# Products of constants ahead of stages and between router products in a four-layer macaron network

## The chip, the cores and the metric

The kernel runs on one core of a Trainium2 chip. The metric is the device time of one execution in microseconds; the time of a kernel is the median of several runs. All data are 32-bit floats.

## What is computed

The reference passes a tensor x of 2 x 512 tokens with 256 features through four layers. Each layer is a feed-forward part, a sequence-mixing part and the same feed-forward part again, each behind a layer norm and added to x, the feed-forward parts at half weight. The parts are:

- Layer 0, feed-forward: a mixture of 32 experts of hidden size 176, 6 for each token, beside a shared gated network of hidden size 352. Sequence part: retention with 16 heads, and a GELU network.
- Layer 1, feed-forward: a linear layer with binarized weights. Sequence part: attention over the keys of those tokens that an importance score selects. The kernel does the whole layer in one stage, l1.
- Layer 2, feed-forward: 8 dense experts, of which the router picks one. Sequence part: a state-space mixer with 8 heads.
- Layer 3, feed-forward: a mixture of 8 experts of hidden size 176, 2 for each token, beside a shared network of hidden size 176. Sequence part: a state-space mixer with 64 heads.

The mixture of experts, which runs four times (twice in layer 0, twice in layer 3), is in short:

```python
scores = softmax(x2d @ wg_router.T)          # layer 3: sigmoid
topk_w, topk_idx = top_k(scores, K)
topk_w = topk_w / (sum(topk_w) + 1e-20)
g = einsum('ecd,edf->ecf', xe, w_gate)        # xe: the tokens of each expert
u = einsum('ecd,edf->ecf', xe, w_up)
ye = einsum('ecf,efd->ecd', silu(g) * u, w_down)
y = weighted sum of each token's K rows of ye
sh = silu(x2d @ ws_gate) * (x2d @ ws_up) @ ws_down
```

## The kernel before, in words

**Tiling.** The 1024 tokens are 8 chunks of 128 (NC = 8, four for each of the two sequences, CB = 4); the 256 features are two blocks of 128 (KD = 2). x stays in the on-chip memory throughout. Each 32-bit product that the program writes is two matmuls in the profile; a transpose, which is a product with the identity matrix, is one. The stages run one after the other, as STAGES lists them (L2072): l0_ffn, l0_attn, l0_ffn, l1, l2_ffn, l2_attn, l2_ffn, l3_ffn, l3_attn, l3_ffn.

**A mixture of experts (moe, L622).** For each sequence, layernorm (L221) makes xn on DVE from a mean and a scale that DVE and POOL work out (L201, L212), xn goes to a table in HBM, and transpose_tokens (L173) turns it with 8 transposes into ps_tr, from which DVE or ACT copies to xT. Then logits (L312) does the router: 8 chunks x 2 feature blocks, into ps_lg, and a DVE copy takes it out (L320). While DVE makes the lists of tokens, shared_unit (L354) runs the shared network, pg and pu first (L365), with DVE's h behind (L369). In this part the order of PE's instructions is the order in which they are written: in_order (L135) chains them.

Then experts_sparse (L506) runs the experts. A unit is an expert with one or two tiles of 128 tokens. POOL gathers the tokens from the table (xe, L527), turn_x (L537) transposes them (ps_xe, L541), hidden does gate and up (ps_gu, L551), turn_h transposes the result (ps_he, L565), down_ multiplies it by the last weight (ps_ye, L576), and POOL writes the rows to HBM (L581). The loop is pipelined over units: turn_x of unit n, turn_h of n - 2, hidden of n - 1, down_ of n - 2. A conditional branch (L688) holds further tiles for an expert that has more tokens than expected; it isn't entered here. The rows of a token are added to x only when the next stage needs them: settle (L159) runs add_rows (L694), which loads y<-rows and adds with DVE (L714) or, in l1, with PE into ps_add (L707).

**The stages behind a mixture of experts.** l0_attn (L767) begins with a norm by chunks (scales, norm), transposes pt_h (L833) and the projections pq. l1 (L1100) begins with add_rows through PE (ps_add), and a loop over chunks that are three steps apart. The state-space mixer (mamba, L1562) serves l2_attn (flag few, 8 heads) and l3_attn (64 heads). It has row (the norm and transposes of one sequence; in l3_attn by_chunks, L259, which takes each chunk as its rows come), decay_sums (L1605: pd, ps_row, ps_cum, ps_dec), convolutions whose projections pp (L1675) PE makes and whose taps DVE adds, products (L1699: pb, pm), prep_front and prep_back (pt, L1757), and z_gate (pz, L1809). The order of its start on PE, ACT and DVE is written out by hand from L1937 on, with in_order around it.

**PSUM.** In the mixture of experts' first part, and in l1 and the mixer, psM has 4 buffers under the tag "mm" that all small products take in turn; the experts have a pool with one buffer for each name.

**Constants.** ident is the 128 x 128 identity, le a 128 x 512 array of zeros and ones; both are loaded once at the start.

Of the kernel before, what the change touches and what calls it, by code (L numbers as in the profile page):

```python
# [10 lines left out]
F32 = mybir.dt.float32  # L11
# [7 lines left out]
P = 128  # L19
B, S, D = 2, 512, 256  # L20
T = B * S
NC = T // P
CB = S // P
# [60 lines left out]
class Net:  # L84
# [69 lines left out]
    def rsqrt(self, out, in_, scale=1.0):  # L154

        self.nc.scalar.activation(out, in_, AF.Sqrt, bias=self.eps, scale=scale)
        self.nc.vector.reciprocal(out, out)

    def settle(self, b, n=CB, psum=None):  # L159


        parts = self.pending.get(b, [])
        while len(parts) > CB - n:
            parts.pop(0)(psum)
        if not parts:
            self.pending.pop(b, None)
# [66 lines left out]
    def layernorm_T(self, es, psum):  # L233


        xT = es.enter_context(self.tc.tile_pool(name="xT", bufs=1)).tile([P, KD, T], F32, name="xT")
        p = es.enter_context(self.tc.tile_pool(name="ln", bufs=1))

        made = {}

        def measure(b):
            made[b] = self.scales(p, b)

        def norm(b):
            made[b] = self.layernorm(p, p.tile([P, CB, D], F32, tag="xn", name="xn"), b, *made[b])

        def turn(b, k):
            self.transpose_tokens(made[b], xT, psum, b, k)

        def row(b):  # L250
            if b in self.pending:
                by_chunks(b)
                return
            measure(b)
            norm(b)
            for k in range(KD):
                turn(b, k)

        def by_chunks(b):  # L259

            xn = p.tile([P, CB, D], F32, tag="xn", name="xn")
            ps = [psum.tile([P, S], F32, tag="mm", name="ps_tr") for _ in range(KD)]
            ms = {}
            for cc in range(CB + 1):
                if cc < CB:
                    self.settle(b, cc + 1)
                    ms[cc] = self.scale(p, b * CB + cc, b * CB + cc)
                if cc > 0:
                    j = cc - 1
                    self.centre(xn[:, j, :], b * CB + j, *ms[j])  # L270
                    for k in range(KD):
                        self.nc.tensor.transpose(
                            ps[k][:, j * P : (j + 1) * P], xn[:, j, k * P : (k + 1) * P], self.ident
                        )
            for k in range(KD):
                self.evac(xT[:, k, b * S : (b + 1) * S], ps[k])

        return xT, row, measure, norm, turn
# [30 lines left out]
        nc.vector.tensor_tensor(gt, gt, eq, ALU.add)  # L309
        return gt  # L310

    def logits(self, pool, psum, xT, wT, e):  # L312
        lg = pool.tile([P, NC, e], F32, name="lg")
        ps = psum.tile([P, NC, e], F32, tag="mm", name="ps_lg")
        for c in range(NC):
            for k in range(KD):
                self.nc.tensor.matmul(  # L317
                    ps[:, c, :], xT[:, k, c * P : (c + 1) * P], wT[:, k, :], start=(k == 0), stop=(k == KD - 1)
                )
        self.nc.vector.tensor_copy(lg, ps)  # L320
        return lg

# [183 lines left out]
    def experts_sparse(self, ew, ps, xes, table, rows, lists, w, ex, f, tiles, per, ahead=4, wp=None):  # L506
# [28 lines left out]
            return xe  # L535

        def turn_x(n, xe, nt):  # L537
            pt = ps.tile([P, KD, nt * P], F32, name="ps_xe")
            for k in range(KD):
                for i in range(nt):  # L540
                    nc.tensor.transpose(pt[:, k, i * P : (i + 1) * P], xe[:, i, k:D:KD], self.ident)  # L541
            xeT = ew.tile([P, KD, nt * P], F32, name=f"xeT{n % 2}")
            self.evac(xeT, pt)
            return xeT
# [25 lines left out]
        def down_(n, e, js, hT, wd):  # L570
            nt = len(js)
            y = ew.tile([P, nt, D], F32, name=f"ye{n % 4}")
            py = ps.tile([P, nt, D], F32, name=f"ps_ye{n % 2}")
            for i in range(nt):
                for q in range(2):
                    nc.tensor.matmul(  # L576
                        py[:, i, :], hT[:, q, i * P : (i + 1) * P], wd[:, q, :], start=(q == 0), stop=(q == 1)
                    )
            self.evac(y, py)
            for i, j in enumerate(js):  # L580
                put_rows = nc.gpsimd.indirect_dma_start(  # L581
                    rows,
                    bass.IndirectOffsetOnAxis(put[:, e * per + j : e * per + j + 1], 0),
                    y[:, i, :],
                    None,
                    bounds_check=last,
                    oob_is_err=False,
                )

                for other in self.puts:  # L590
                    self.tc.declare_no_dep(put_rows.ins, other.ins, reason="no two slots have one row")
                self.puts.append(put_rows)
# [29 lines left out]
    def moe(self, pre, names, E, F, K, FS, PER, tiles, cap, r, scores, scale):  # L622
# [6 lines left out]
        with ExitStack() as es:  # L629
# [7 lines left out]
            with ExitStack() as fs:  # L637
# [6 lines left out]
                with tc.tile_pool(name="ln", bufs=1) as lp:  # L644
                    tv = table[:, :D].rearrange("(b c p) d -> b p c d", p=P, b=B)
                    rT = self.router_weights(sb, psM, router, E)
                    tail = {}
                    with self.in_order(tail, ("PE",)):
                        for b in range(B):
                            xn = lp.tile([P, CB, D], F32, name=f"xn{b}")  # L650
                            self.layernorm(lp, xn, b, *self.scales(lp, b))
                            nc.scalar.dma_start(tv[b], xn)
                            for k in range(KD):
                                self.transpose_tokens(xn, xT, psM, b, k)
                        s = self.logits(sb, psM, xT, rT, E)
                if cap < T:

                    zero = lists.tile([P, D], F32, name="zero")
# [108 lines left out]
    def l0_attn(self):  # L767
# [10 lines left out]
        with ExitStack() as es:  # L778
# [252 lines left out]
                    nc.vector.tensor_tensor(self.x[:, c, :], self.x[:, c, :], py, ALU.add)  # L1031


            for c in range(2):
                scales(c)
            norm(0)
            w2 = self.w("fc1")[:, : KD * F].rearrange("p (k f) -> p k f", k=KD)
            nc.sync.dma_start(w2, a[pre + "fc1_w"].rearrange("(k p) f -> p k f", p=P))
            w3 = self.w("fc2")[:, : NF * D].rearrange("p (c d) -> p c d", d=D)
# [60 lines left out]
    def l1(self):  # L1100
# [19 lines left out]
        with ExitStack() as es:  # L1120
# [173 lines left out]


            with tc.tile_pool(name="a1m", bufs=4, space=PSUM) as psM:
                for c in range(NC + 4):
                    if c < NC:
                        front(c)
                    if c == CB:  # L1300
                        wt = self.w("w4")[:, : KD * 4 * D].rearrange("p (k n d) -> p k n d", k=KD, n=4)
                        for n, name in enumerate(("Wq", "Wk", "Wv", "Wo")):
                            nc.sync.dma_start(wt[:, :, n, :], a[pre + name].rearrange("(k p) d -> p k d", p=P))
                    if 0 <= c - 1 < NC:
                        turn_x(c - 1)
                    if 0 <= c - 2 < NC:
                        back(c - 2)
                    if 0 <= c - 3 < NC:
                        measure(c - 3)
                    if c >= 4:  # L1310
                        norm(c - 4)
                    if c == 1:
                        nc.gpsimd.tensor_copy(wib, wi.to_broadcast([P, KD, P]))
                        nc.vector.tensor_scalar(bqs, bq, DH**-0.5, None, ALU.mult)
                    if c == CB + 4:
                        importance(0)
                        for m in range(KD):
                            queries(0, m)
                    elif c > CB + 4:
                        for i in range(2):  # L1320
                            if 2 * (c - CB - 5) + i < CB:
                                ranks(0, 2 * (c - CB - 5) + i)
# [239 lines left out]
    def mamba(self, pre, win, wout, nh):  # L1562
# [14 lines left out]
        with ExitStack() as es:  # L1577
# [27 lines left out]
            def decay_sums(b):  # L1605
# [29 lines left out]
                nc.vector.tensor_scalar(t1, d, 1e-18, None, ALU.max)  # L1635
                nc.scalar.activation(jb[:, bs, :], t1, AF.Ln)
                yield

                cr = wk.tile([nh, 2, S], F32, tag="cr", name="cr", bufs=1)
                ps = psM.tile([nh, S], F32, tag="mm", name="ps_row")  # L1640
# [56 lines left out]
                return conv(wb[:, :, P : 2 * P], NX + 1, b, CT[:, b * S : (b + 1) * S])  # L1697

            def products(b):  # L1699
                pb = psM.tile([P, CB, P], F32, tag="mm", name="pb")  # L1700
                pm = psM.tile([P, CB, P], F32, tag="mm", name="pm")
                for cc in range(CB):
# [49 lines left out]
                return taps, rest  # L1752

            def prep_back(u, m):
                pt = psM.tile([P, CB, P], F32, tag="mm", name="pt")
                for cc in range(CB):
                    nc.tensor.transpose(pt[:, cc, :], u["xc"][:, m, cc * P : (cc + 1) * P], self.ident)  # L1757
                nc.scalar.copy(u["xt"][:, :, m * P : (m + 1) * P], pt)  # L1758

                n = u["g"] * NM + m  # L1760
                nc.scalar.mul(u["xc"][:, m, :], u["xc"][:, m, :], dcol[:, n : n + 1])
# [173 lines left out]
            later = {}  # L1935
            tail = {}
            with self.in_order(tail, ("PE", "Activation", "DVE")):  # L1937
                row(0)
                fetch_wx(*order[0])
                d0, d1 = decay_sums(0), decay_sums(1)  # L1940
# [178 lines left out]
```

## Time and profile before

| | us |
|---|---|
| median of three runs | 2031.36 (2030.21 to 2033.29) |
| the profiled execution | 2029.85 |
| its span, first to last instruction | 2028.0 |
| PE busy | 1762.7 (87%) |
| DVE busy | 1131.6 (56%) |
| POOL busy | 903.5 (45%) |
| ACT busy | 800.6 (39%) |
| mean granted TensorE clock | 0.917 |

PE is TensorE, PEld its weight loads, which run beside matmuls; DVE is VectorE, ACT is ScalarE, POOL is GpSimd. In the page's second part each digit is the busy share of one fortieth of the span in tenths, and PEclk is the clock that TensorE was granted, in tenths of full speed. In a row of the timeline the first two numbers are start and length in us, then engine, line, operation, what it writes and from what, shape and count, and in brackets how long the engine had been idle before it and what ended that. A row for a stretch of time has, after the stretch and its length, the busy us of PE, PEld, DVE, ACT and POOL with the instructions in brackets, then the granted clock, the share of the DMA engines and GB/s.

The heaviest groups are the experts' products: ps_gu (L551) with 704 matmuls and 232.5 us, ps_ye (L576) with 704 and 168.3 us; in the mixer pp (L1675) with 288 and 144.9 us and pz (L1809) with 1152 and 144.4 us. The router's six calls wait 39.4 us in all for ps_lg, which counts DVE's time in front of its copies.

### The profile page before, as it was taken

The numbers are of one execution on the slowest core, as the hardware profiler recorded it, in microseconds if no ns is written. First come the engines' busy times: TensorE is split into PE (matmuls) and PEld (weight loads), VectorE is DVE, ScalarE is ACT, GpSimd is POOL, SyncE is SP. The second block draws the span as 40 slices with busy tenths as digits, with TensorE's granted clock in tenths as the row PEclk, the third lists the DMA queues.
The fourth block names the chain that finished last, engine by engine and source line by source line (L and its number), as shares of the span: only waits on it lengthen the run. The fifth ranks groups of instructions, "written<-read, shape, count | busy, mean of one in ns | idle before, by whom it ended". The sixth has DMA issues, their size and how long they took to land. (4 is left out here: it accounts for less than half of the span.)

```text
span 2028.0 us, 29711 instructions
## 1 busy us (share of the span) xinstructions
PE 1762.7 (87%) x10662; PEld 1259.7 (62%) x10662; DVE 1131.6 (56%) x2657; ACT 800.6 (39%) x1342; POOL 903.5 (45%) x889
## 2 busy tenths in 40 slices
PE   5899769888999678798788989589999899999895
PEld 4677636565777545444465367357777677777564
DVE  4533276217333476556563653578777677777443
ACT  1132224211232144301751013268777677777111
POOL 3477655311777421100240026135657456667253
PEclk8999989889999789889897979689999999999798
DMA  8266440051565500000220013434454444444133
GB/s 310 80 187 189 153 173 12 16 162 33 170 184 172 209 22 1 22 0 17 100 83 22 11 40 97 131 125 156 152 167 146 154 138 154 160 151 130 44 96 95
DMA packets 117441, 226.49 MB, mean 112 GB/s; under 512 B 22383, under 2 KB 68829, under 8 KB 117015
## 3 DMA queue, kind: packets, MB, share of 16 engines
q1 hardware_dynamic: 88134, 170.17, 26.2%
q0 software_dynamic: 20608, 48.45, 7.6%
q10 hardware_dynamic: 8528, 5.72, 0.9%
q8 instruction: 93, 1.52, 0.3%
q14 instruction: 78, 0.63, 0.1%
HBM read 195.59 MB, written 41.81 MB: 117 GB/s over the span
## 5 line engine op out<-in xcount | busy, mean ns | idle before, releaser
L527 POOL DMA_INDIRECT xe<-table,sl_get x176 | 179.9, 1022 | 202.0 <-DVE sl_get L503 148.1
L551 PE MATMUL ps_gu<-we,xeT 128*128 128x352 f32 x704 | 232.5, 472 | 0.0
L581 POOL DMA_INDIRECT rows<-ye,sl_put x176 | 177.0, 1006 | 83.7 <-issue 40.5
L1682 DVE SCALAR_TENSOR_TENSOR xc<-pp,L_attn_cols,xc 128x511 f32<-128x511 f32 (+2 forms) x216 | 161.4, 747 | 34.7 <-ACT xc L1678 29.4
L576 PE MATMUL ps_ye<-we,hT 88*128 88x256 f32 x704 | 168.3, 379 | 2.9 <-ACT ye L132 1.6
L556 DVE SCALAR_TENSOR_TENSOR he<-se,xe,ps_gu 128x176 f32<-128x176 f32 x176 | 69.9, 397 | 180.2 <-ACT se L555 169.1
L551 PEld LDWEIGHTS ps_gu<-we,xeT 128*128 128x128 f32 x704 | 130.0, 196 | 56.5 <-issue 5.5
L576 PEld LDWEIGHTS ps_ye<-we,hT 88*128 88x128 f32 x704 | 133.0, 190 | 37.0 <-ACT ye L132 3.6
L1809 PE MATMUL pz<-xT,wt 128*128 128x128 f32 x1152 | 144.4, 279 | 11.9 <-ACT xt L1758 5.5
L1785 DVE SCALAR_TENSOR_TENSOR lm<-lm,jb,top 128x128 f32<-128x128 f32 x576 | 153.6, 340 | 0.0
L1675 PE MATMUL pp<-xT,wx 128*128 128x512 f32 x288 | 144.9, 628 | 5.6 <-issue 2.4
L1809 PEld LDWEIGHTS pz<-xT,wt 128*128 128x128 f32 x1152 | 137.8, 195 | 17.0 <-issue 9.6
L1882 PE MATMUL yacc<-wt,y 128*128 128x256 f32 x576 | 144.4, 394 | 0.7 <-POOL y L1864 0.7
L1864 POOL TENSOR_TENSOR y<-y,sg 128x512 f32<-128x512 f32 x72 | 91.7, 1274 | 106.8 <-DVE y L1863 105.2
L1802 POOL TENSOR_TENSOR ce<-ce,CT 128x1024 f32<-128x1024 f32 x54 | 127.9, 2369 | 0.0
L1882 PEld LDWEIGHTS yacc<-wt,y 128*128 128x128 f32 x576 | 104.8, 191 | 24.2 <-issue 10.8
L1514 PE MATMUL ps_y<-w8T,xT 128*128 128x512 f32 x256 | 118.9, 619 | 0.0
L555 ACT ACTIVATE se<-ps_gu 128x176 f32<-128x176 f32 x176 | 55.9, 318 | 154.0 <-PE ps_gu L551 153.9
L1837 PE MATMUL py<-lm,xt 128*64 128x128 f32 x1152 | 108.0, 281 | 8.0 <-issue 6.5
L1875 POOL TENSOR_TENSOR sqs<-sqs,sq 128x512 f32<-128x512 f32 x56 | 71.4, 1275 | 89.4 <-ACT sq L1874 89.4
L1794 DVE TENSOR_TENSOR lm<-lm,M 128x1024 f32<-128x1024 f32 x72 | 87.1, 1215 | 42.7 <-ACT lm L1790 41.1
L217 POOL TENSOR_SCALAR ln_rstd<-ln_mv 128x4 f32<-128x4 f32 x15 | 3.5, 236 | 238.2 <-DVE ln_mv L209 227.5
(401 smaller groups left out, 3478.6 us busy)
## 6 DMA issues: line engine op xcount, KB each, us to landing
lm<-rows SPq DMA_DIRECT2D x72, 512.0 KB
ce<-rows SPq DMA_DIRECT2D x54, 512.0 KB
rows<-zero POOLq DMA_DIRECT2D x16, 768.0 KB, 11.8
y<-rows SPq DMA_DIRECT2D x16, 768.0 KB
we<-in_L_ffn_w_gate_dram SPq DMA_DIRECT2D x64, 176.0 KB
we<-in_L_ffn_w_up_dram SPq DMA_DIRECT2D x64, 176.0 KB
we<-in_L_ffn_w_down_dram SPq DMA_DIRECT2D x64, 176.0 KB
we<-in_L_ffn_w_dram SPq DMA_DIRECT2D x48, 176.0 KB
```

Source lines behind the costliest of these rows:

```text
L527: nc.gpsimd.indirect_dma_start(xe[:, i, :], None, table, bass.IndirectOffsetOnAxis(get[:, e * per + j : e * per + j + 1], 0), bounds_check ...
L551: nc.tensor.matmul(pg, xeT[:, k, i * P : (i + 1) * P], wgu[:, :, k], start=(k == 0), stop=(k == KD - 1))
L576: nc.tensor.matmul(py[:, i, :], hT[:, q, i * P : (i + 1) * P], wd[:, q, :], start=(q == 0), stop=(q == 1))
L581: put_rows = nc.gpsimd.indirect_dma_start(rows, bass.IndirectOffsetOnAxis(put[:, e * per + j : e * per + j + 1], 0), y[:, i, :], None, bou ...
L1514: nc.tensor.matmul(ps, xT[:, k, cs], self.w8T[:, k, 2 * e2 : 2 * e2 + 2, :], start=(k == 0), stop=(k == KD - 1))
L1675: nc.tensor.matmul(pp, wv[:, k, :], xT[:, k, b * S : (b + 1) * S], start=(k == 0), stop=(k == KD - 1))
L1682: nc.vector.scalar_tensor_tensor(out[:, 3 - w :], pp[:, : S - 3 + w], cw[:, m, w : w + 1], out[:, 3 - w :], ALU.mult, ALU.add)
L1785: nc.vector.scalar_tensor_tensor(k["lm"][:, h, :], k["lm"][:, h, :], jb[:, k["c"], n : n + 1], top, ALU.add, ALU.min)
L1802: nc.gpsimd.tensor_tensor(k["ce"], k["ce"], ct, ALU.mult)
L1809: nc.tensor.matmul(pz[:, m, :], u["wz"][:, kk, m * P : (m + 1) * P], xT[:, kk, c * P : (c + 1) * P], start=(kk == 0), stop=(kk == KD - 1),)
L1837: nc.tensor.matmul(py[i * HP : (i + 1) * HP, m, :], w[:, h * HP : (h + 1) * HP], v[:, h, :], start=(m == 0 and n == 0), stop=(n == len(src ...
L1882: nc.tensor.matmul(yacc[cc // 2][:, cc % 2, :], k["y"][:, m, :], u["wo"][:, m, :], start=(u["g"] == 0 and m == 0 and cc % 2 == 0), stop=(u ...
```

## The change

A new method, warm, issues n products of the identity with 256 columns of le into a PSUM tile that nobody reads. It is called:

- in moe: 4 products before each sequence's norm and transposes, and one after each router chunk but the last;
- in experts_sparse: 2 before and 2 after the transposes of the first unit;
- at the start of l0_attn: 22, and 4 after the first chunk's norm;
- at the start of l1: 18;
- in the mixer: 4 (l2_attn) or 18 (l3_attn) at the start, one between chunks in by_chunks, 4 in the first decay_sums before ps_row, 4 before the first products, 8 before the third prep_back.

In all 177 products are executed (those in the branch at L688 are not), that is 354 matmuls of 256 columns.

```diff
+    def warm(self, psum, n, tag="mm", w=256):
+        ps = psum.tile([P, S], F32, tag=tag, name="warm")
+        for _ in range(n):
+            self.nc.tensor.matmul(ps[:, :w], self.ident, self.c["le"][:, :w], start=True, stop=True)
...
                     self.centre(xn[:, j, :], b * CB + j, *ms[j])
+                    if j < CB - 1:
+                        self.warm(psum, 1)
...
-    def logits(self, pool, psum, xT, wT, e):
+    def logits(self, pool, psum, xT, wT, e, warm=False):
...
+            if warm and c < NC - 1:
+                self.warm(psum, 1)
         self.nc.vector.tensor_copy(lg, ps)
...
         def turn_x(n, xe, nt):
+            if n == 0:
+                self.warm(ps, 2, tag="ps_ye1")
             pt = ps.tile([P, KD, nt * P], F32, name="ps_xe")
...
+            if n == 0:
+                self.warm(ps, 2, tag="ps_ye1")
             xeT = ew.tile([P, KD, nt * P], F32, name=f"xeT{n % 2}")
...
-            py = ps.tile([P, nt, D], F32, name=f"ps_ye{n % 2}")
+            py = ps.tile([P, nt, D], F32, tag=f"ps_ye{n % 2}", name=f"ps_ye{n % 2}")
...
                         for b in range(B):
+                            self.warm(psM, 4)
                             xn = lp.tile([P, CB, D], F32, name=f"xn{b}")
...
-                        s = self.logits(sb, psM, xT, rT, E)
+                        s = self.logits(sb, psM, xT, rT, E, warm=True)
...
+            self.warm(psM, 22)
             for c in range(2):
                 scales(c)
             norm(0)
+            self.warm(psM, 4)
...
             with tc.tile_pool(name="a1m", bufs=4, space=PSUM) as psM:
+                self.warm(psM, 18)
                 for c in range(NC + 4):
...
+                if b == 0:
+                    self.warm(psM, 4)
                 cr = wk.tile([nh, 2, S], F32, tag="cr", name="cr", bufs=1)
                 ps = psM.tile([nh, S], F32, tag="mm", name="ps_row")
...
             def products(b):
+                if b == 0:
+                    self.warm(psM, 4)
...
             def prep_back(u, m):
+                if u["b"] == u["g"] == 0 and m == 2:
+                    self.warm(psM, 8)
...
             with self.in_order(tail, ("PE", "Activation", "DVE")):
+                self.warm(psM, 4 if few else 18)
                 row(0)
```

In the instruction streams the PE order stays as it was apart from the added products, which stand exactly at these places; the waits of the branch at L688 come ahead of the fills. On DVE, ACT and POOL a few neighbours change places: in l0_attn, ACT's second chunk of the first norm stands ahead of the first hT copy, and DVE's first t product behind the norm of a later chunk. SP's order is the same.

## The prediction

> **What bounds the kernel now.** I read the first two parts of the page, then the work and granted clock of single stretches (windows), then the timeline around each place where the change puts work.
>
> ```profile
> span 2028.0 us, 29711 instructions
> PE 1762.7 (87%) x10662; PEld 1259.7 (62%) x10662; DVE 1131.6 (56%) x2657; ACT 800.6 (39%) x1342; POOL 903.5 (45%) x889
> PE   5899769888999678798788989589999899999895
> PEclk8999989889999789889897979689999999999798
> ```
>
> PE is busy 87% of the span, and no other engine passes 56%. The dips of the clock row lie in the slices where PE's own row dips, at stage borders. The mean clock is 0.917; with only 1.0 and 0.5 granted, (1 - 0.917) x 2 x 2028 = 337 us ran at half. The next fence has stretches: length, busy us of each engine, and, after POOL, the granted clock.
>
> ```profile
> 100.00:200.00 100.00, 100.00 (x482) 78.92 (x481) 36.59 (x70) 30.25 (x70) 76.95 (x76) 1.00 0.63 190
> 450.50:457.40 6.90, 6.90 (x34) 6.90 (x34) 0.09 (x1) 1.87 (x2) 0.00 (x0) 0.50 0.21 68
> 507.10:511.90 4.80, 4.80 (x12) 2.75 (x11) 0.40 (x1) 0.90 (x2) 3.58 (x5) 0.52 0.32 89
> 684.00:689.30 5.30, 5.30 (x13) 4.15 (x14) 3.89 (x8) 0.00 (x0) 1.53 (x3) 0.51 1.01 415
> ...
> 1169.00:1172.60 3.60, 3.60 (x19) 3.60 (x18) 1.66 (x4) 0.59 (x1) 2.74 (x6) 0.50 0.44 150
> 1172.60:1179.40 6.80, 6.80 (x34) 6.80 (x33) 0.08 (x1) 0.59 (x1) 0.00 (x0) 0.50 0.00 0
> ...
> 1292.80:1300.20 7.40, 7.32 (x21) 5.26 (x22) 1.37 (x5) 2.29 (x5) 0.00 (x0) 0.50 0.20 73
> 1302.00:1341.00 39.00, 24.64 (x78) 14.60 (x76) 27.78 (x55) 25.33 (x37) 2.29 (x2) 0.74 0.46 142
> ```
>
> Inside the experts PE has no idle time and full clock; each stage's first products run at half. The timeline tells what they are, and who waits:
>
> ```profile
> 450.51 6.87 PE L317 MATMUL ps_lg<-routerT,xT 128*128 128x32 f32 x32
> ...
> 457.19 3.59 PE L365 MATMUL pg<-xT,wsh 128*128 128x512 f32 x4
> ...
> 462.61 0.69 DVE L369 SCALAR_TENSOR_TENSOR h<-s,pu 128x512 f32<-128x512 f32 x1 [1.38 <-PE pu L365]
> ...
> 507.18 4.76 PE L551 MATMUL ps_gu<-we,xeT 128*128 128x352 f32 x8
> ...
> 684.00 5.38 PE L707 MATMUL ps_add<-y,cst 128*128 128x256 f32 x12 [13.01 <-DMA y<-rows]
> ...
> 1287.06 0.66 PE L272 MATMUL ps_tr<-cst,xn 128*128 128x128 f32 x2 [12.88 <-DVE xn L198]
> ```
>
> **How the clock moves in this trace.** It changes only on a grid of 3.41 us that runs on through the kernel. I took, for each grid window, the time in which columns stream, and the clock of the next one. At full clock, windows up to about 0.38 busy (0.36 to 0.43 is uncertain) were followed by half; at half, those from 0.76 up mostly by full, those to 0.75 never. Between them the state keeps itself. [...] A matmul of 256 columns streams 0.213 us at full and 0.427 at half, so a warm product costs 0.427 or 0.853.
>
> **Part 1: warm products between router chunks (7 in each of 4 MoE calls), and 4 + 4 before the transposes.** The 32 matmuls of a call take 6.87 us, 0.21 each: the weight load sets them, and 32 columns (or 8) stream almost nothing. Here a rule speaks against the change. The Trainium skill, "TensorE: Matmul & The Clock Gate", Part 1 (The HAM clock gate), releases the throttle after about 3.4 us of sustained activity. If these back-to-back matmuls counted as that, the router would need 3.4 at half + 1.7 at full = 5.1 us, and the 7 warm ones (3.0 us at full) would only be added: +1.2 against today, in each call. The row has 0.50 for the whole 6.90 us, so I count streamed columns. Then at full clock: 32 x 0.107 + 7 x 0.427 = 6.4 us, busy share about 0.5, which holds the clock. That is 0.4 us less than now; the gain is what follows: pg and pu run at full at once, and DVE's wait for pu (1.38 + 0.73 us here, 2.2, 2.0 and 3.1 us in the first, third and fourth call) goes. At half: 6.87 + 7 x 0.853 = 12.8 us, again about 0.5 to 0.6 busy, so it doesn't recover: +6 us.
>
> Which state is there is decided by the transposes and 4 + 4 warms ahead. That page's Part 4 (PE-mode transpose) says that transposes don't engage the full clock; then in the first call, where only transposes run from 16 to 20.3 us, the clock could not rise. There, pairs of transposes went from 0.43 us at 17 to 20, and the records have full clock from 20.17. So transposes count here, and 8 of them with 4 + 4 warms fill a window. By the rule the routers would more often start at half (+6 each); by the trace they start at full in three of four.
> - Call 1 (0 to 48 us): warms lie in idle PE time (10.8 to 16); ACT's late copies of xT set the logits' end, so -2.0.
> - Call 2: logits done 0.5 us earlier, waits gone, pg/pu at full: -2.7.
> - Call 3 (1169 us): the 16 transposes are contiguous, and warms stand on the path: 3.67 us of transposes and 8 x 0.853 = 6.8 us of warms, 5 of the 10.5 us at half and the rest at full = 7.7, so +4.0; less 0.4, less 2.5 of pg/pu: +1.1.
> - Call 4: the first four warms push transposes by 1.2, hidden before the second batch; -2.6.
>
> Sum -6.2 with all at full. Each call at half instead loses its 2 to 2.7 and adds 6: about +8.2.
>
> **Part 2: 2 + 2 warms around an MoE call's first turn_x.** The first unit's 8 gate/up matmuls took 4.76 us here (0.59 each; the steady rate is 0.293). They are the head of a chain that PE bounds, as the row of 100 to 200 us shows, so what they save carries through. At full they take 2.35; the first two warms lie in the wait for gathers, the later two (0.85 us at full) beside the copy of xeT (0.7 us). By call: 81.3 to 85.5, 507.2 to 511.8, 1212.3 to 1215.9, 1943.4 to 1948.1 us: -2.3, -3.0, -1.5, -2.4, together -9.2. Four warms are 1.7 us of a window; with the transposes around them not always 0.76. I take -7.5. If they stay at half: the later pair 1.7 us, 1 of it on the path, +4 in all.
>
> **Part 3: fills ahead of attention stages.** PE sits there for y<-rows; it passes the overflow branch 7 to 14 us before its data.
> - l0_attn, 22 + 4: from 247.5; the first 3.4 to 6.8 us at half, the rest at full: 18.8 us of half-rate work ends at 259 to 260, and the data come at 261.4. pt_h and pq (266.6 to 269.7) save 1.5; but the order of instructions moves ACT's h(1) ahead of hT(0), and DVE's t(0) behind the second chunk's norm (some 1.5 to 2.6 us later). I take 0 (-1.5 to +1.5).
> - l1, 18: from 674.9, ends 684.3 to 686.0, against data at 684.0: +1.1; ps_add and the next transposes 5.38 to 2.7: -2.6. DVE waited 0.18 for ps_add, so part only: -1.5.
> - l2_attn, 4 + 4 + 4 + 8: between DVE's and ACT's taps, in idle PE; pp at 961 and pt/pz at 993 save 1.7 and 1.6, pb/pm little. A warm before ps_row may hold it 0.5: -3 (0 to -5).
> - l3_attn, 18 + 3 + 4 + 4 + 8: the 18 run 1277.7 to about 1288; transposes come at DVE's pace until 1291.6, so 1 us late is hidden. pd and pp (1292.9 to 1301.7, 8.8 us, 7.4 at half) save 3.5; of the later 39 us, at 0.74, PE is on the chain for some 5 us of half-clock work: -2.5. Sum -6 (-1 to -10).
>
> Part 3 is -10.5. DVE, ACT and POOL otherwise do the same work; SP's order, and so every load, is unchanged. A warm waits for a free PSUM buffer, whose copies the next product needs anyway; behind it waits PE's next instruction only.
>
> **Sum.** -6.2 - 7.5 - 10.5 = -24 us with every router at full; with one of four at half, -16. I take -20 against the profiled 2029.85 us (span 2028.0), that is 2009.9; the median lies 1.5 above the profile: 2011.
>
> **Rivals.**
> 1. The covers bind. DMA, DVE and ACT set the stage starts (27.8 us of DVE and 25.3 of ACT in the 39 us at 1302), and shorter PE pieces only wait longer. Part 3 gives 0, part 2 half: -6 - 4, +8 for one router at half: about 2029.
> 2. Slower: every router starts its logits at half. Place: the gap between the two batches' transposes (446.8 to 448.4, 1899 to 1901.4) and the late xT of call 1 leave a window under 0.38. Price 8.2 us a call: -24 + 8.2 n. From n = 3 the gain is gone; at 4 it is +9, 2040. For it: the first call's last window ahead of its logits was 0.39 by my count, and the next was half. Against: warms add 0.4 to 1.7 us to those windows.
> 3. All goes to plan and all of it lies on the path: about 125 us of half-clock PE work in the places addressed, halved: 1969. Against it: waits for DMA and DVE end there.
> 4. The gate doesn't count these products: 4 x 6 + 4 + some 6 at starts: 2065. Against: ps_add, also identity times data, raised the clock at 689.2.
>
> **Numbers.** Likeliest case 0.68 (1996 to 2022); rival 1 0.17; rival 2 0.08; rival 3 0.04; rival 4 0.03. The three runs before spread 0.15%, so 0.2% (4 us) is about what can be told from no change. Faster by more: most of 0.68, half of rival 1, rival 3: 0.80; within: 0.10; slower: 0.10. The range takes in rival 1 and the better end of the likeliest: 1990 to 2034.
>
> **What will show it.** Mean clock near 0.95 or above; logits groups of 6.4 us with pg/pu at 0.43 us a matmul (right), or 12.8 us (rival 2); gu0 near 2.4 us; ps_add 2.7 us; pd/pp after 1293 in about 5 us. I am wrong if pieces shorten and the next wait lengthens by as much, or if the warms of l1 or l3_attn outlast their data by over 2 us.

## The result, and the profile after

The changed kernel takes 2020.82 us (median of 4 runs, 2019.02 to 2023.24) against 2031.45 us: ratio 0.9948, 95% interval 0.9930 to 0.9965. The forecast was 2011, between 1990 and 2034: faster, as forecast, with half of the gain. The profiled execution took 2022.34 us with a span of 2020.0.

The page after has the same rows as before. PE is busier by 53 us (354 added matmuls are 75 us at full clock; the rest runs faster), and the mean clock went from 0.917 to 0.945:

```profile
span 2020.0 us, 30430 instructions
PE 1815.6 (90%) x11016; PEld 1310.3 (65%) x11016; DVE 1130.3 (56%) x2657; ACT 800.0 (40%) x1342; POOL 904.7 (45%) x889
...
PE   6899979799999878799788989889999899999895
PEclk8999989899999889889997989899999999999898
```

By the sum that the prediction used, half clock is left for (1 - 0.945) x 2 x 2020 = 222 us instead of 337. The stretches of the second call's router, of its first gate/up products, of ps_add, of the third call's transposes, router and first gate/up products, and two of l3_attn's start (columns as before: stretch, length, busy us of PE, PEld, DVE, ACT, POOL, granted clock, DMA share, GB/s):

```profile
453.70:460.10 6.40, 6.40 (x48) 6.04 (x46) 0.42 (x1) 1.87 (x2) 0.00 (x0) 1.00 0.25 84
507.80:510.20 2.40, 2.40 (x11) 1.56 (x10) 0.40 (x1) 0.90 (x2) 1.97 (x2) 1.00 0.36 98
684.20:686.90 2.70, 2.70 (x14) 2.32 (x14) 2.25 (x4) 0.00 (x0) 1.50 (x1) 1.00 1.02 428
1165.90:1173.60 7.70, 7.70 (x33) 6.63 (x33) 1.14 (x4) 0.58 (x1) 2.72 (x6) 0.67 0.20 70
1173.70:1180.10 6.40, 6.40 (x47) 6.04 (x46) 0.40 (x1) 0.59 (x1) 0.00 (x0) 1.00 0.00 0
1212.20:1216.10 3.90, 3.90 (x10) 2.34 (x10) 0.40 (x1) 0.69 (x2) 2.92 (x4) 0.60 0.27 79
1292.90:1300.60 7.70, 7.70 (x22) 4.82 (x23) 1.87 (x5) 2.71 (x5) 0.00 (x0) 0.56 0.13 45
1300.60:1338.60 38.00, 29.43 (x113) 18.91 (x111) 28.36 (x56) 25.48 (x37) 2.24 (x2) 0.91 0.47 146
```

The router ran at full clock, as forecast: from its first product to pg it took 6.5 us (the row cuts it at 6.4). Eight gate/up matmuls took 2.4 us instead of 4.8, ps_add 2.7 instead of 5.3. But the third call's transposes and warm products took 7.7 us where transposes alone took 3.6, its first gate/up products are still at 0.60, and l3_attn's pd and pp (last row but one) are back at 0.56 in spite of the fill before them. The stretch behind them (last row) went from 0.74 to 0.91.

To see where time went I took the start of the same instruction in both traces, and the change of that distance from stage to stage. All are differences after minus before, in us, and sum to the -8.0 of the spans:

| stretch | forecast | measured |
|---|---|---|
| call 1, start to first turn_x | -2.0 | +2.5 |
| its experts | -2.3 | -2.7 |
| l0_attn, from the last ps_ye of call 1 | 0 | +4.0 |
| call 2, start to first turn_x | -2.7 | -1.6 |
| its experts | -3.0 | -3.9 |
| l1 and most of l2_ffn | -1.5 | -1.2 |
| l2_attn, with the end of l2_ffn | -3 | -0.3 |
| call 3, start to first turn_x | +1.1 | +1.9 |
| its experts | -1.5 | +1.4 |
| l3_attn | -6 | -1.9 |
| call 4, start to first turn_x | -2.6 | -2.5 |
| its experts | -2.4 | -3.7 |

The experts' stretches give -8.9, all four routers together nothing (+0.3), the attention stages nothing (+0.6). Two things limit this table. It holds one trace against one. And the border between "start to first turn_x" and "its experts" lies behind two of the added products. The second call shows what they do to it, before and after:

```profile
498.37 1.18 POOL L527 DMA_INDIRECT xe<-table,sl_get  x1 [50.46 <-DVE sl_get L503]
501.92 0.36 PE L541 MATMUL ps_xe<-cst,xe 128*128 128x128 f32 x1 [1.31 <-DVE x L393]
...
499.80 1.18 POOL L538 DMA_INDIRECT xe<-table,sl_get  x1 [48.21 <-DVE sl_get L514]
503.24 1.10 PE L164 MATMUL warm<-cst 128*128 128x256 f32 x4 [1.20 <-DVE x L404]
504.18 1.00 PE L554 MATMUL ps_xe<-cst,xe 128*128 128x128 f32 x4
```

The first transpose follows the first gather after 4.4 us instead of 3.6: it waits for the two products. In three calls this is 0.8 us, in the third 0.2. Counted from the first gather instead, the experts' stretches give -6.2 (-1.9, -3.0, +1.6, -2.9 by call) and the routers -2.4.

In l0_attn the loss is a wait that was not there. The timeline of PE, DVE and ACT around the second chunk's projection, before and (below the dots) after the change:

```profile
269.88 0.59 ACT L849 COPY raw<-pq 128x512 f32<-128x512 f32 x1 [2.41 <-PE pq L843]
270.50 0.69 DVE L857 TENSOR_TENSOR t<-pq,tab 128x512 f32<-128x512 f32 x1
271.61 1.88 PE L843 MATMUL pq<-w,hT 128*128 128x512 f32 x4
...
274.05 0.56 ACT L865 COPY raw<-pq 128x512 f32<-128x512 f32 x1
274.65 0.69 DVE L873 TENSOR_TENSOR t<-pq,tab 128x512 f32<-128x512 f32 x1 [0.81 <-ACT raw L865]
275.39 2.61 PE L859 MATMUL pq<-w,hT 128*128 128x512 f32 x4 [3.22 <-DVE t L873]
```

The first three rows are the copies of the first chunk's pq and the second pq; the others are the same three. Now ACT and DVE take the norms of later chunks first, and PE waits 3.2 us for the PSUM buffer that holds pq.

### The profile page after: what moved, and what is told of

Its sections match the earlier page's. It is cut to its first block, busy times and chain, and to the rows that moved or that the text cites. A ratio compares the mean times of both kernels' runs of the same rounds, so it can differ in the third digit from the quotient of the medians.

```text
span 2020.0 us, 30430 instructions
## 1 busy us (share of the span) xinstructions
PE 1815.6 (90%) x11016; PEld 1310.3 (65%) x11016; DVE 1130.3 (56%) x2657; ACT 800.0 (40%) x1342; POOL 904.7 (45%) x889
## 5 line engine op out<-in xcount | busy, mean ns | idle before, releaser
L566 PE MATMUL ps_gu<-we,xeT 128*128 128x352 f32 x704 | 226.4, 462 | 0.0
L1696 PE MATMUL pp<-xT,wx 128*128 128x512 f32 x288 | 138.4, 604 | 3.4 <-ACT dec L1687 0.9
L164 PE MATMUL warm<-cst 128*128 128x256 f32 x354 | 106.9, 448 | 16.7 <-PEq L704 5.9
```

Of the source, the lines that this page charges most:

```text
L566: nc.tensor.matmul(pg, xeT[:, k, i * P : (i + 1) * P], wgu[:, :, k], start=(k == 0), stop=(k == KD - 1))
L1696: nc.tensor.matmul(pp, wv[:, k, :], xT[:, k, b * S : (b + 1) * S], start=(k == 0), stop=(k == KD - 1))
```

## The experiments

Each run was compared with the kernel before on the same chip. The chips differ: on the first, on that of the ninth and tenth run and on that of the last two, the kernel before takes 2029 to 2031 us; on that of the first four runs and that of the next four it takes 2113 us, the experts of the two 32-expert calls taking some 30 us longer each, those of the 8-expert calls 7 to 14. There TensorE is no longer the bound of the experts: run 4's row for 100 to 200 us has it busy for 90.8 us of 100, where the prediction's row has 100.

```profile
100.00:200.00 100.00, 90.79 (x406) 69.24 (x405) 29.93 (x58) 23.83 (x58) 67.55 (x67) 0.95 0.52 160
```

Comparisons between totals are therefore made within a chip. Those between stages use the distances in the traces, and the only trace of the kernel before is that of the first chip. Such distances scatter: from the second call's last ps_ye to the third call's ps_rt, where runs 2, 4 and 7 add nothing, they take 3.5 us more, 1.6 less and 3.8 more than before. So single entries of 1 to 2 us are hints at most.

**1. Without l0_attn's fills** (the chip of 2113 us).

```diff
-            self.warm(psM, 22)
...
-            self.warm(psM, 4)
```

> The change without the 22 + 4 products of l0_attn. Theory A (the fills of l0_attn cost about 4 us, because with them DVE and ACT take their work in another order: the first raw<-pq copy waits behind later norms and hT copies, and PE then waits 3.2 us for the second pq): about 2016.5 us, 4 us under the whole change, and the second pq of l0_attn follows the first within some 4 us again as before. Theory B (the 4 us come from the rows landing later, or from the phase of the clock's grid, and the fills help): as the whole change or slower, 2020 to 2024 us.

Ratio to before 1.0003 (0.9987 to 1.0019). From its first transposes to its end l0_attn is 0.2 us shorter than in the profile before, against 3.6 longer with the fills: the distance speaks for A. The second pq follows the first after 6.3 us, against 5.0 before and 7.8 with the fills, so that sign came only half-way. The total did not show a gain on this chip.

**2. Only the MoE calls' products.** All calls in attention stages removed.

> Only the products in the four MoE calls (before transposes, between router chunks, around the first turn_x), none in the attention stages. Theory A (MoE part gives the gain, the attention fills nothing on balance): segments of the profiles add up to about -9, so 2022 us. Theory C (the products on the router's path cost what the experts' heads gain, and the gain is from the attention fills): 2029 to 2032 us.

Ratio 1.0008 (0.9990 to 1.0026). The first call's router fell to half 0.5 us after its start and took 12.4 us; its pg 6.2 us later after ps_rt than before.

**3. Only the attention fills.** All calls in moe and experts_sparse removed.

> Only the fills of l0_attn, l1, l2_attn and l3_attn. Theory A: l0_attn +4.2, l1 -1.3, l2_attn -0.3, l3_attn -1.9: about 2032 us. Theory C: 2020 to 2023 us.

Ratio 0.9988 (0.9969 to 1.0008). l0_attn 2.0 us longer, the start of l3_attn, from the third call's last ps_ye to its first pz, 3.9 shorter; the experts' first gate/up matmuls take 3.7 to 4.6 us, as before. Neither theory's total is told apart.

**4. Only the products around the first turn_x.**

> Only the 2 + 2 products around the first turn_x of each MoE call. Theory A (the experts' heads carry the gain: 8 gate/up matmuls at full clock in 2.5 instead of 4.8 us, three or four times): -7 to -9, 2022 to 2024 us. Theory D (the clock of the heads hangs on the whole part before, and 4 products alone don't fill a grid window to 0.76): -2 to 0, 2029 to 2031 us.

Ratio 1.0028 (1.0011 to 1.0045). In all four calls the eight matmuls take 2.53 us: D is wrong about the clock. Yet the time did not fall on this chip, which neither theory explains.

**5. The whole change again,** on a second chip of 2113 us.

> The whole change once more, beside the three kernels below on one chip. If the experts are bound by TensorE as in the first profile: ratio to the kernel before 0.995. If this chip's experts wait for data instead (the four runs before ran on a chip on which the kernel before took 2113 us and the experts' stretches were 30 us longer): the gain of the experts' heads is swallowed, ratio 0.998 to 1.001. All theories share this.

Ratio 1.0011 (0.9985 to 1.0036), the second case. Both the first and the second call's routers fell to half. The second one in this run, to be held against 453.70:460.10 above:

```profile
487.30:499.30 12.00, 12.00 (x47) 10.74 (x45) 0.35 (x1) 1.87 (x2) 0.00 (x0) 0.52 0.13 45
```

**6. l0_attn's fills in fewer, wider products,** with the old order on the other engines.

```diff
-            self.warm(psM, 22)
+            self.warm(psM, 5, w=512)
...
-            self.warm(psM, 4)
+            self.warm(psM, 1, w=512)
```

> The whole change, but l0_attn's 22 and 4 products of 256 columns are 5 and 1 of 512 columns: fewer, so that DVE, ACT and POOL keep the order that they had before the change in l0_attn. Theory A (the order costs the 4 us): 3 to 4 us less than the whole change, and pq of the second chunk starts at most 1 us later against the first than in the kernel before. Theory B (the products in front of the first transposes cost it, or the clock): as the whole change, within 1 us.

Ratio 1.0025 (1.0003 to 1.0047). The second pq starts 5.8 us after the first, against 5.0 before and 7.8 with the change; l0_attn as a whole is 1.7 us longer instead of 3.7 in the run beside it. So about 2 us go to the order or to the shorter filling, for the six wider products also stream less than half the columns of the 26 (3072 against 6656). Other stretches of this run lost more than that.

**7. Once more only the products around the first turn_x.**

> Again only the 2 + 2 products around the first turn_x, the router and attention stages as before. Theory A: the heads run at full clock in most calls, xe0 to the third unit's transposes shortens by 2.5 to 4 us a call; where the experts are bound by TensorE -7 to -9 us in all, 0.9960. Theory D (4 products do not raise the clock by themselves): heads shorten by under 1 us a call, ratio 0.999 to 1.000.

Ratio 1.0019 (1.0002 to 1.0036). Again 2.53 us in each call; the second call's, to be held against 507.18 in the prediction:

```profile
538.26 2.53 PE L564 MATMUL ps_gu<-we,xeT 128*128 128x352 f32 x8
```

From the second call's first turn_x to its third unit 3.4 us are gained, against 3.5 with the whole change in run 5.

**8. Without l0_attn's fills and the first and third call's router products.**

```diff
+                            if self.calls in (2, 4):
-                            self.warm(psM, 4)
+                                self.warm(psM, 4)
...
-                        s = self.logits(sb, psM, xT, rT, E, warm=True)
+                        s = self.logits(sb, psM, xT, rT, E, warm=self.calls in (2, 4))
```

> The change without l0_attn's fills, and with the products before transposes and between router chunks in the second and fourth MoE call only, where they cost nothing in the profile (in the first and third they held the transposes up by 2.3 and 1.9 us on balance). Theory A: 4 + 4 us less than the whole change, ratio about 0.991 where the experts are bound by TensorE. Theory B and C: no better than the whole change.

Ratio 0.9972 (0.9954 to 0.9991): the only one of the eight with a gain on these chips, and 0.4% under the whole change beside it, with intervals that just overlap.

**9. The same products with 8 columns instead of 256** (the chip of 2030 us).

```diff
-    def warm(self, psum, n, tag="mm", w=256):
+    def warm(self, psum, n, tag="mm", w=8):
```

> The whole change with products of 8 instead of 256 columns: as many, at the same places, but each streams a thirty-second of the time (l0_attn keeps its old order with them, because they are short). If the gain is the clock's (all theories but E): the clock stays at 0.917, the heads of the experts stay at half (5 us), the router at 6.9 to 7.5 us, and the ratio is 0.999 to 1.002. Theory E (the changed order of other instructions, or the mere presence of matmuls, makes the difference): the heads shorten, and the time moves as with the whole change.

Ratio 1.0121 (1.0106 to 1.0135): slower by 24 us, which none of the theories had. The clock stayed at 0.917 and the experts' heads at 3.9 to 4.9 us, so it is the streaming that raises it, not the presence of matmuls. But a product of 8 columns is not free. The second call's router (its row and its timeline), and its first gate/up products:

```profile
453.00:463.00 10.00, 10.00 (x49) 10.00 (x48) 0.46 (x1) 1.87 (x2) 0.00 (x0) 0.50 0.16 54
453.38 0.90 PE L326 MATMUL ps_lg<-routerT,xT 128*128 128x32 f32 x4
454.09 0.57 PE L164 MATMUL warm<-cst 128*128 128x8 f32 x2
454.52 1.04 PE L326 MATMUL ps_lg<-routerT,xT 128*128 128x32 f32 x4
...
512.60 4.84 PE L566 MATMUL ps_gu<-we,xeT 128*128 128x352 f32 x8
```

From one to the next, the pair of tiny matmuls takes 0.43 us at half clock, and PEld is busy without a break (10.00 of 10.00 us): the weight loads set the pace. 7 of them add 3.0 us to a router. From ps_rt to pg the four calls are 14 us longer together, and l2_attn 5. In l0_attn, where the other engines keep their old order, this run loses 0.4 us.

**10. Only what paid.** As run 8, with the router products in the fourth call alone, and without l2_attn's first 4.

```diff
-                            self.warm(psM, 4)
+                            if self.calls == 4:
+                                self.warm(psM, 4)
...
-                self.warm(psM, 4 if few else 18)
+                if not few:
+                    self.warm(psM, 18)
```

> The products kept only where no profile shows them to cost: around the first turn_x of all four MoE calls, before transposes and between router chunks in the fourth call alone, at the start of l1, and in the mixers (in l2_attn without the 4 at the start). Theory A with rival 2 of the prediction (the routers of the first and second call fall to half in some executions and then lose 4.5 to 6 us): the loss is gone, ratio 0.992 to 0.996 on any chip, and narrower than the whole change. If the gain needs the router's products in front of the heads: 0.999.

Ratio 0.9955 (0.9938 to 0.9971). The gain doesn't need the products of the first three routers, but this is no better than the whole change. In its profile l3_attn's first pz comes 7.8 us earlier in the span than before, and then its steady part, which holds no added product, is 9.2 us longer. The two rows, before and in this run:

```profile
1337.80:1894.20 556.40, 538.56 (x4024) 416.99 (x4024) 417.09 (x885) 407.40 (x561) 348.50 (x256) 0.99 0.45 144
1330.00:1895.60 565.60, 542.75 (x4024) 422.01 (x4023) 416.66 (x885) 407.29 (x561) 348.70 (x256) 0.98 0.43 142
```

**11. As run 10, with the third call's router products too.**

```diff
-                            if self.calls == 4:
+                            if self.calls >= 3:
```

> As the version before (only what paid), but with the third MoE call's products before transposes and between router chunks as well. These cost 1.9 us by the profiles. But in all four profiles of kernels without them (and with the products around turn_x) the long steady part of l3_attn, which holds no added product, was 7 to 9 us longer, with the mixer's wt loads landing about 1 us later each, and in the others it was not. Theory F (that stretch hangs on the program as a whole, and comes back to its old length with these products): 7 us less than the version before, ratio about 0.992. Theory G (it was chance): 2 us more than the version before, ratio 0.996 to 0.997.

Ratio 0.9967 (0.9953 to 0.9982), as G said; the steady part of l3_attn is 5.2 us longer, between the two.

**12. The whole change a third time,** beside run 11.

> The whole change a third time, for the state of the routers in the first and second call and for l0_attn. All theories: l0_attn 3.5 us longer than before from its first transposes to its end; the first call's router at half clock with 5 to 7 us lost in most executions, the second's in about half of them (4.7 us), the fourth's never; ratio 0.994 to 0.997 where the experts are bound by TensorE, 1.000 where they are not.

Ratio 0.9964 (0.9949 to 0.9980), in agreement with the first result. Its four routers in order, where the first lost 6.1 us and the others ran at full clock (the rows leave out the edges of the routers):

```profile
25.60:37.80 12.20, 12.20 (x45) 10.94 (x45) 0.00 (x0) 0.58 (x1) 1.61 (x3) 0.50 1.03 412
454.80:461.00 6.20, 6.20 (x45) 5.84 (x45) 0.26 (x1) 1.87 (x2) 0.00 (x0) 1.00 0.26 87
1174.40:1180.50 6.10, 6.10 (x44) 5.74 (x44) 0.18 (x1) 0.51 (x1) 0.00 (x0) 1.00 0.00 0
1903.20:1909.50 6.30, 6.30 (x46) 5.95 (x45) 0.00 (x0) 1.87 (x2) 0.00 (x0) 1.00 0.17 61
```

l0_attn is 1.8 us longer here, from its first transposes on, not the 3.5 that were expected.

## Why the forecast was right in direction and twice too large

The parts of the forecast were -6.2, -7.5 and -10.5 us; by the table they gave +0.3, -8.9 and +0.6. One of three came. That the sum still lies inside the likeliest case (1996 to 2022), at its edge, owes much to the width of that case.

**The rule of the clock held.** From its first product to pg, a router at full clock took 6.5 us with the products, one at half 11.8 to 12.8. A router that fell did so within its first 1.2 us and stayed down, save in the first profile, where a wait of 1.1 us for xT inside the first call's router made the clock fall in its middle. Run 9 shows that streamed columns raise the clock, and that the back-to-back router matmuls don't.

**Part 2 was right in mechanism and near in size.** -7.5 forecast; -8.9 measured from the first transpose, -6.2 from the first gather. From the gathers on, the four stretches took 501.5 us before and 501.1 in run 9, but 494.0 in run 12 and 492.0 and 491.2 in runs 10 and 11, all on chips of 2030 us. On the chips of 2113 us they took 583.2 in run 3, without these products, and 578 to 586 with them: no gain to be told there.

The eight matmuls of the first, second and fourth call became 1.9, 2.2 and 2.4 us shorter, which is what the intervals in the prediction give (4.2, 4.6 and 4.7 less 2.35); its own list of -2.3, -3.0, -1.5 and -2.4 adds to 9.2 where these intervals hold 7.7. Wrong was that the first two products lie in the wait for gathers: they hold the first transpose up by 0.8 us in three calls. Four products suffice, without the router's ahead: 2.53 in all calls of runs 4, 7 and 10, where 2.35 was worked out. Only the third call's head is uncertain: 4.0 to 4.2 us in the first profile and in runs 2 and 12, no faster than without any, 3.1 in run 8 and 2.53 in the others, the same program being on either side. In the first profile this cost 1.4 where 1.5 of gain was forecast.

**Part 1 failed at "they start at full in three of four" and at "Call 1: ... -2.0".** The fourth call was right each time (-2.5 to -2.9 in nine profiles), and the third (+1.9; +4.1 at the start, -2.2 given back). The first call was at half through most or all of its router in five of the five further profiles with these products (runs 1, 2, 5, 6, 12) and lost 5.7 to 7.0 us; the first profile, half of it, 1.9. The second call was at half in two of seven (+4.6 and +4.7 at pg), else -0.8 to -0.9. This is rival 2 of the prediction, with its price (6 us) and its place right, in one or two calls instead of four.

Counted in the prediction's way, the grid window ahead of or around the first call's first product was only 0.00 to 0.35 busy in those five profiles, because PE waits there for ACT's late copy of xT (3.9 us in run 5). The second call stands on the edge: the window in which its router begins was 0.37 to 0.43 busy in five of seven profiles, inside the range that the prediction calls uncertain, and two of these five fell.

In the first call, fills have little to gain in any case: ACT's second copy of xT ends at 28.8 us in both profiles, and the products behind it stand on the path (from there to pg 3.1 us before, 5.1 after). The prediction's 0.39 for that call's last window before the change isn't found: in the window from 20.2 us PE is busy for 0.36 us of 3.4.

**Part 3 failed in two ways.** For l0_attn the step "I take 0 (-1.5 to +1.5)" saw the changed order and under-priced it: t(0) moved by 4.1 us, not 1.5 to 2.6, because ACT's raw copy, on which it waits, moved too. Four traces with fills and the changed order lost 1.8 to 3.7 us from the first transposes on, run 6 with the old order 1.7, and of the traces without fills six -0.3 to +0.1 and one 1.4: the order is a cause, but not the only one. The second pq came 7.8 us after the first in all four traces with the changed order, and 4.8 to 6.4 in the ten others. For the mixers the pieces were counted at full clock where it fell again: in l3_attn the 18 products ran to 1288.9, but the transposes and the 3 single products after them filled too little of a window, and pd and pp fell to half once more (0.56 above); at most 0.8 was gained there (at pp) where 3.5 was forecast. The later stretch came as forecast: from the first ps_row to the first pz 29.3 us instead of 31.5 (-2.2, forecast -2.5). In l2_attn the 4 products before the transposes, at 940.8, stand on their path and cost 1.8 us, which took back what the later ones gained (2.0).

**What stays open.** Runs 8, 10 and 11 leave out what cost time and gain it back stage by stage until l3_attn, whose steady part is then 5 to 9 us longer; so it is in runs 4 and 7 (7 to 8 us), on other chips, and not in the other traces (3.0 or less). The five have one thing in common: products around turn_x, but none at the first call's router. The traces account for the length, though not for its origin. In the five, TensorE stands idle 2.4 to 5.6 us longer in this part than before, and 3 to 11 us more of its work run at half clock, which costs half of that; the two together make up the excess of each within 0.4 us. What starts the waits isn't known; in runs 4, 7 and 10 ACT waits 25 us for the mixer's weights wt, against 20 before, but in runs 8 and 11 only 23.4 and 22.6.

Why the totals on the chips of 2113 us show no gain is known in part only. In runs 4 and 7 this longer part takes about as much as the heads can give, in runs 1, 2, 5 and 6 the first call's router does (5.7 to 7.0 us), and TensorE isn't the experts' bound there. No run has the products around turn_x alone on a chip of 2030 us, so what they give to a total by themselves isn't measured. No version here is shown to beat the change: run 10 has 0.9955, with an interval that overlaps both results of the whole change.

## What to carry to other kernels

Filling products are best placed where a dense, TensorE-bound chain follows at once: two before and two after a first transpose nearly halved the time of its first matmuls in every call of seven of the eleven traces with them at full width, and in three of four calls of the others. Whether the total falls was another matter: it did on the chips where TensorE is the bound, not on the others. Between small matmuls they make two self-keeping states, and the wrong one costs more (4.6 to 7.0 us) than the right one gains (0.8 to 2.9 us in the second and fourth call); look first at what the window ahead of them holds. And look at the order that the other engines get: products that nobody reads moved a copy by 4 us on engines that they don't use.

## What was not expected of the hardware

- A matmul of 8 columns costs its weight load: 0.21 us each at half clock, as much as a transpose of 128 columns there.
- The same program took 2029 to 2031 us on some chips and 2113 on others, nearly all of the difference being in the experts' stretches, where TensorE is the bound on the first.
- The clock never left its two values, and the time between its changes was a multiple of 3.41 us up to the end of the span.
